# Masked attention, then an int8 linear layer: the last half in single steps, more row sums on the array, int8 loads in twos

## The chip, the cores and the metric

The kernel runs on one core of one Trainium2 chip. The time is the device time of one execution in microseconds (us); the median of three executions is compared. All stage times below are counted from the start of the span of one profiled execution. In the profile PE is the matrix engine (PEld its weight loads), DVE the vector engine, ACT the scalar engine, POOL the GpSimd engine and SP the queue from which this kernel issues nearly all of its transfers.

## The reference

`x` is (8, 512, 1024): 8 batches, 512 channels, 1024 positions. Cut to what matters, and with the int8 step written out:

```python
Q, K, V = (einsum('oc,bct->bto', W, x).reshape(B, T, 16, 32).transpose(0, 2, 1, 3) for W in (Wq, Wk, Wv))
att = einsum('bhqd,bhkd->bhqk', Q, K) / sqrt(32) + b[0]
att = softmax(att * m + (1 - m) * -1e30)          # m: 0/1 mask over the keys
y   = einsum('bhqk,bhkd->bhqd', att, V)           # back to (B, 512, 1024)
scale = max(abs(y).max(-1), 1e-7) / 127           # one scale for each row of 1024
q   = clip(round(y / scale), -128, 127)           # int8
out = x + (einsum('bsk,nk->bsn', q, weight) * scale * w_scale + bias).astype(float16)
```

So each of the 8 x 512 rows of the attention's result must be known over all its 1024 positions before it can be rounded, and only then can the linear layer (1024 in, 1024 out) of that row start.

## The kernel before

**Groups, halves, steps, pairs.** The work is cut into 32 groups (a batch and four of its 16 heads, that is 128 channels). A group has two halves of 512 queries, a half has 8 steps of 128 keys (kc 0 to 7), so there are 512 steps. The main loop (L783 to L844) runs over pairs of steps, 8 pairs p = 0 to 7 in a group i, with four pairs for each half. Nothing is reordered by a planner: the order in which the Python calls are made is the order on every engine's queue (`manual_schedule`), and the framework only adds the waits. Each queue is strictly in order, SP and POOL included.

**One step.** `scores(s)` (L407) makes 4 matmuls that spread the shift, which is the row maximum (L418), and 4 matmuls of keys by queries (L423) into two PSUM tiles from a pool `ps_s` of two buffers; ACT then takes the exponential of each of the two tiles (L432) into `e`, which has three buffers. `product(s)` (L450) multiplies the `e` of that step by the values into `av` (L457). The sum of the exponentials, the softmax denominator, is made by POOL: `add_up` (L437) adds one `e` after another into `sum` (7 adds in a half, L444), and matmuls with a matrix of ones add up its rows once a half (`half_denominators`, `add_rows`, L471 to L492). In the very last half the row sums are made on the array directly from each `e`, with no POOL add (`last_denominators`, L496).

**Pairs.** In a pair the order on PE is: scores of step s; then `product` of the two steps of the pair before; then scores of step s+1; then four units of `maxima` (L334), which find row maxima two halves ahead (PE makes 1024 scores for 128 queries, DVE takes their maximum, L375), with "pieces" of a job between them: projections of the groups ahead, or the linear layer of two groups back. Two of the four units use the buffers of `ps_s`, so they wait for ACT or DVE to free them. The maxima of a half are split into bf16 parts by POOL (`split_tops`, L389, five small instructions) and turned by a transposing DMA (`place_tops`, L398); the first shift matmul of that half needs this transfer.

**The int8 weights.** In groups 0 and 1 eight blocks of the weight matrix are loaded by SP (`load_ffn`, L151), one at the start of each of the pairs 0, 1, 4 and 5, and cast to bf16 by POOL two at a time at the start of the pairs 2 and 6 (`casts`, L157). On POOL the casts stand between adds of the sum; on SP the loads stand between the copies that build the operands of `maxima` (`stack_head`, L315) and the weight loads of the projections (`load_w`, L111). `load_w` of Wq is queued after pair 4's units and its first user is the first piece of pair 5.

**The end.** Group 31 is the last. Its maxima were all made by its pair 2. The linear layer of group 29 runs in its pairs 1 and 2, that of group 30 in its pairs 6 and 7. After the loop: row sums and products of the last two steps, division (four reciprocals on DVE, L510), the largest value, the scale, rounding of the two halves on ACT (two instructions each, L537 and L539), 8 transposes on PE (L578), clipping on DVE (L573), the linear layer of group 31 in two halves one after the other (L614), each followed by three DVE instructions (scale L626, bias L598, add `x` L599) and its store; both halves' `x` is loaded at the moment the half's first matmul is queued (L590).

Of the kernel before, what the change touches and what calls it, by code (L numbers as in the profile page):

```python
# [20 lines left out]
P = 128  # L21
# [11 lines left out]
def kernel(  # L33
# [49 lines left out]
    last = n_groups - 1  # L83
    SCALE = 1.0 / math.sqrt(DH)
# [352 lines left out]
    def add_up(s):  # L437
        X, kc = divmod(s, NT)
        if kc == 0 or X == n_halves - 1:
            return  # L440
        if kc == 1:
            sums[X] = work.tile([P, HG, HALF], F32, tag="sum", name=f"sum_{X}", bufs=2)
        other = exps[s - 1] if kc == 1 else sums[X]
        nc.gpsimd.tensor_tensor(sums[X], other, exps[s], ALU.add)  # L444
# [32 lines left out]
    def take_denominators(X, acc):  # L477
        dens[X] = work.tile([P, HALF], F32, tag="den", name=f"den_{X}")
        nc.vector.tensor_copy(dens[X], acc)

    def denominators(X):
        acc = bank(f"dps_{X}")
        add_rows(acc, sums.pop(X), True, True)
        take_denominators(X, acc)

# [8 lines left out]
    last_sum = []  # L494

    def last_denominators(s):  # L496

        kc = s % NT
        if kc == 0:
            last_sum.append(ps_m.tile([P, HALF], F32, tag="m", name="dps_last"))  # L500
        add_rows(last_sum[0], exps[s], kc == 0, kc == NT - 1)
        if kc == NT - 1:
            take_denominators(n_halves - 1, last_sum[0])
# [29 lines left out]
    def round_y(i, step, cols=slice(0, T)):  # L533
        inv, _, qt = quants[i]
        y = ys[i][:, cols]
        if step == 0:
            nc.scalar.activation(y, y, AF.Identity, bias=rounding[:, 0:1], scale=inv)  # L537
        else:
            nc.scalar.activation(qt[:, cols], y, AF.Identity, bias=rounding[:, 1:2])  # L539

    def quantise(i, step):
# [6 lines left out]
        if step == 1:  # L548
            nc.scalar.activation(y, y, AF.Identity, bias=rounding[:, 0:1], scale=inv)
            nc.scalar.activation(y, y, AF.Relu, bias=rounding[:, 2:3])  # L550
        else:
            nc.scalar.activation(y, y, AF.Relu, bias=rounding[:, 3:4], scale=-1.0)
# [12 lines left out]
    def last_turn(i):  # L565

        pieces = NH
        _, scale, qt = quants.pop(i)
        tr = bank(f"qtps_{i}", BF, (P, NT, P))
        qT = work.tile([P, NT, P], BF, tag="qT", name=f"qT_{i}")  # L570

        def rest(ks):
            nc.vector.tensor_scalar(qT[:, ks, :], tr[:, ks, :], -128.0, 127.0, ALU.max, ALU.min)  # L573

        for a in range(pieces):
            ks = slice(a * NT // pieces, (a + 1) * NT // pieces)
            for k in range(ks.start, ks.stop):
                nc.tensor.transpose(tr[:, k, :], qt[:, k * P : (k + 1) * P], ident)  # L578
            later.append(lambda ks=ks: rest(ks))
        outs[i] = qT, scale  # L580

    def linear(i, h, quarters=(0, 1), width=QUARTER):

        b, g = divmod(i, NG)
# [3 lines left out]
        def begin():  # L588
            xr = work.tile([P, HALF], F32, tag=f"xr{h}", name=f"xr_{i}_{h}")
            nc.sync.dma_start(xr, x[b, g * P : (g + 1) * P, half])  # L590
            o = work.tile([P, HALF], F32, tag=f"o{h}", name=f"o_{i}_{h}")
            o16 = work.tile([P, HALF], F16, tag=f"o16{h}", name=f"o16_{i}_{h}")
            residual[i, h] = xr, o, o16

        def finish():
            xr, o, o16 = residual.pop((i, h))
            engine = nc.vector if i == last else nc.gpsimd
            engine.tensor_tensor(o16, o, bias_sb[:, half], ALU.add)  # L598
            engine.tensor_tensor(o, o16, xr, ALU.add)  # L599
            store = lambda: nc.sync.dma_start(out[b, g * P : (g + 1) * P, half], o)  # L600
            if i == last:
                store()
            else:
                stores.append(store)

        def piece(a, r):
            if (i, h) not in residual:
                begin()
# [4 lines left out]
            for k in range(r * size, (r + 1) * size):  # L613
                nc.tensor.matmul(  # L614
# [16 lines left out]
            if a == HALF // width - 1:  # L631
                finishes.append(finish)

        return [lambda a=a, r=r: piece(a, r) for a in quarters for r in range(NT // size)]


# [30 lines left out]
    def job(i, p):  # L667


        if i == last:  # L670
            if p in (1, 2):
                return linear(i - 2, p - 1, (0,), HALF)
            if p in (6, 7):
                return linear(i - 1, p - 6, (0,), HALF)
            return []
# [27 lines left out]
    def after_units(i, p):  # L703

        flush(stores)
        if i == last:
            if p == 3:
                for step in range(HN):
                    normalise(2 * i - 1, step)
            if p == 4:  # L710
                normalise(2 * i - 1, 4)
                quantise(i - 1, 0)
                quantise(i - 1, 1)
            if p == 5:
                quantise(i - 1, 2)
# [61 lines left out]

    load_mask(0)
# [4 lines left out]
    for n in range(FIRST, n_pairs):  # L783
# [23 lines left out]
        if i in (0, 1) and p in (0, 1, 4, 5):  # L807
            load_ffn(i * HG + (0, 1, 4, 5).index(p))
# [3 lines left out]
        if n >= 1:  # L812
            for a in (s - 2, s - 1):
                if a >= n_steps - NT:
                    last_denominators(a)
                product(a)
# [5 lines left out]
        if p == 5 and i == last:  # L822
# [93 lines left out]
```

## Time and profile before

| | |
|---|---|
| Median of three executions | 2579.47 us (2577.87 to 2584.42) |
| Profiled execution: time | 2581.33 us |
| Profiled execution: span | 2579.5 us, granted PE clock 0.994 |
| PE busy | 2516.9 us, 98% |
| POOL busy | 2259.7 us, 88% |
| DVE busy | 1801.7 us, 70% |
| ACT busy | 1477.8 us, 57% |
| PE busy in the stretch 60 to 220 us | 145.45 of 160 us |
| PE busy in the stretch 500 to 2000 us | 1496.24 of 1500 us |
| PE busy in the stretch 2510 to 2556 us | 37.28 of 46 us, clock 0.89 |
| PE busy in the stretch 2556 to 2579.5 us | 6.78 of 23.5 us, clock 0.72 |

How to read it: PE is full in the middle of the run, from about 220 us to about 2510 us. It has gaps in groups 0 and 1 (60 to 220 us) and in the second half of group 31 with what follows (from 2510 us on). A line of the timeline has the start, the duration, the engine, the source line, the operation with its output and inputs, how many were merged, and in brackets how long the engine had been idle before it and what ended that wait.

### The profile page before, as it was taken

Reading aid. Unit: us, or ns where it says so; the run is one execution under the profiler, and the core shown is the slowest. Engines: PE = TensorE matmul, PEld = TensorE weight load, DVE = VectorE, ACT = ScalarE, POOL = GpSimd, SP = SyncE. Lnnn points to the kernel's source line nnn. Section 1 sums busy time; section 2 is a strip of 40 time slices with the busy share of each in tenths; the row PEclk is TensorE's granted clock in tenths of the full one; section 3 lists DMA queues with packets and bytes.
Section 4 is the critical chain, followed back from the end, with each engine's and each line's share of the span. In section 5 each row is a group of like instructions: output and inputs, shape, how many; then the busy total and the mean of one; then the engine's idle time right before and its main releaser. Section 6 shows DMA issues by size and latency. Waiting matters only on the chain. (4 is left out here: it accounts for less than half of the span.)

```text
span 2579.5 us, 50764 instructions
## 1 busy us (share of the span) xinstructions
PE 2516.9 (98%) x19390; PEld 1426.8 (55%) x19390; DVE 1801.7 (70%) x2886; ACT 1477.8 (57%) x1645; POOL 2259.7 (88%) x911
## 2 busy tenths in 40 slices
PE   8899999999999999999999999999999999999986
PEld 4455555555555555555555555555555555555531
DVE  4466777777777777777777777777777777777772
ACT  2445655565655656655656655656655566555553
POOL 1798899998999999899999999999899998999992
PEclk9999999999999999999999999999999999999998
DMA  4323433334333333334333343334333334233221
GB/s 130 104 54 81 113 84 90 78 84 121 78 83 97 88 100 91 76 91 116 80 80 94 83 115 88 77 79 104 104 86 86 76 88 125 75 87 85 73 54 43
DMA packets 225952, 228.08 MB, mean 88 GB/s; under 512 B 104368, under 2 KB 138160, under 8 KB 225712
## 3 DMA queue, kind: packets, MB, share of 16 engines
q1 hardware_dynamic: 225712, 224.85, 34.1%
q8 instruction: 155, 2.54, 0.4%
q14 instruction: 85, 0.70, 0.1%
HBM read 57.70 MB, written 16.78 MB: 29 GB/s over the span
## 5 line engine op out<-in xcount | busy, mean ns | idle before, releaser
L444 POOL TENSOR_TENSOR sum<-sum,e 128x2048 f32<-128x2048 f32 x378 | 1725.5, 4565 | 31.0 <-ACT e L432 11.8
L375 DVE CUSTOM_DVE_ANT_0 rest<-mps,row 128x1024 bf16<-128x1024 f32 x1024 | 1253.8, 1224 | 627.9 <-PE mps L344 390.6
L432 ACT ACTIVATE e<-sps,kbias 128x1024 f32<-128x1024 f32 x1024 | 1085.7, 1111 | 491.7 <-PE sps L423 468.2
L344 PE MATMUL mps<-ks,qs 128*128 128x512 f32 x2032 | 764.7, 457 | 9.1 <-ACT e L432 5.1
L423 PE MATMUL sps<-qf,kf 32*128 32x512 f32 x4096 | 552.3, 591 | 0.0
L457 PE MATMUL av<-e,v 128*32 128x512 f32 x4096 | 496.5, 602 | 0.0
L344 PEld LDWEIGHTS mps<-ks,qs 128*128 128x128 f32 x2032 | 332.7, 190 | 239.1 <-issue 96.7
L444 POOL TENSOR_TENSOR sum<-e,e 128x2048 f32<-128x2048 f32 x63 | 286.3, 4545 | 157.3 <-ACT e L432 147.0
L457 PEld LDWEIGHTS av<-e,v 128*32 128x32 f32 x4096 | 107.7, 109 | 350.0 <-issue 350.0
L293 PEld LDWEIGHTS job<-wv,x 128*128 128x128 f32 x1860 | 255.7, 191 | 27.5
L293 PE MATMUL job<-wv,x 128*128 128x128 f32 x1860 | 257.8, 274 | 0.0
L418 PE MATMUL sps<-shift,ones_b 32*128 32x512 bf16 x2048 | 233.8, 383 | 20.9 <-DMA shift<-part 11.1
L207 PE MATMUL job<-x,wq 128*128 128x256 f32 x900 | 245.0, 382 | 6.6 <-DMA wq<-in_wqT 6.2
L510 DVE RECIPROCAL den<-den 128x128 f32<-128x128 f32 x256 | 228.4, 925 | 0.0
L207 PE MATMUL job<-x,wk 128*128 128x256 f32 x854 | 223.8, 378 | 0.0
L423 PEld LDWEIGHTS sps<-qf,kf 32*128 32x128 f32 x4096 | 207.8, 184 | 4.4
L207 PEld LDWEIGHTS job<-x,wq 128*128 128x128 f32 x900 | 169.6, 190 | 45.1 <-DMA wq<-in_wqT 12.4
L301 ACT COPY v<-job 128x256 f32<-128x256 f32 (+1 forms) x93 | 41.3, 444 | 251.0 <-PE job L293 251.0
L418 PEld LDWEIGHTS <-ones_b 32*128 32x128 bf16 x2048 | 69.8, 91 | 204.2 <-issue 176.7
L207 PEld LDWEIGHTS job<-x,wk 128*128 128x128 f32 x854 | 161.2, 189 | 30.8
L236 ACT ACTIVATE qh<-job,top 128x256 fp32r<-128x256 f32 (+1 forms) x84 | 47.9, 570 | 170.5 <-PE job L207 169.3
L614 PE MATMUL job<-w_sb,qT 128*128 128x256 bf16 (+1 forms) x960 | 133.0, 278 | 0.0
(97 smaller groups left out, 1429.8 us busy)
## 6 DMA issues: line engine op xcount, KB each, us to landing
ks<-kh SPq DMA_DIRECT2D x512, 64.0 KB, 2.0
ks<-kl SPq DMA_DIRECT2D x512, 64.0 KB, 2.0
qs<-qh SPq DMA_DIRECT2D x508, 64.0 KB, 2.0
qs<-ql SPq DMA_DIRECT2D x508, 64.0 KB, 2.0
x<-in_x SPq DMA_DIRECT2D x32, 512.0 KB, 4.7
xr<-in_x SPq DMA_DIRECT2D x64, 256.0 KB, 3.4
out<-o SPq DMA_DIRECT2D x64, 256.0 KB, 3.4
wk<-in_wkT SPq DMA_DIRECT2D x32, 256.0 KB, 3.7
```

Of the source, the lines that this page charges most:

```text
L207: matmul(acc[:, place], w[:, c, :], x_sb[b, c][:, h * HALF : (h + 1) * HALF][:, cols], start=(c == 0), stop=(c == NG - 1),)
L236: nc.scalar.activation(dst, acc, AF.Copy, scale=top)
L293: matmul(acc[:, place : place + P], x_sb[b, c][:, k * P : (k + 1) * P], wv_sb[:, c, g * P : (g + 1) * P], start=(c == 0), stop=(c == NG - 1),)
L344: nc.tensor.matmul(acc[:, a, :], q[:, n0 * P : (n0 + 1) * P], kk[:, a * HALF : (a + 1) * HALF], start=True, stop=True,)
L375: nc.vector.tensor_tensor_reduce(out=rest, in0=acc.rearrange("p h t -> p (h t)"), in1=row, scale=-1.0, scalar=HIGH, op0=ALU.add, op1=ALU.m ...
L418: nc.tensor.matmul(accs[j // 2][:, j % 2, :], ones_b[r, :], shift[r, :], start=True, stop=False)
L423: nc.tensor.matmul(accs[j // 2][:, j % 2, :], k[r, k0 * P : (k0 + 1) * P], q[r, :], start=False, stop=True,)
L432: nc.scalar.activation(e[:, 2 * a : 2 * a + 2, :], acc, AF.Exp, bias=kbias[:, kc : kc + 1], scale=SCALE)
L444: nc.gpsimd.tensor_tensor(sums[X], other, exps[s], ALU.add)
L457: nc.tensor.matmul(accs_av[X][r, :], v_sb[i][:, kc, r], exps[s][:, j, :], start=(kc == 0), stop=(kc == NT - 1),)
L510: nc.vector.reciprocal(piece, piece)
L614: nc.tensor.matmul(acc, qT[:, k, :], w8_sb[:, k, half][:, cols], start=(k == 0), stop=(k == NT - 1),)
```

## The change

1. **Int8 loads in twos.** The blocks are loaded two at a time, at the start of the pairs 0 and 4 of groups 0 and 1, instead of one each at 0, 1, 4 and 5. The casts stay where they were.
2. **Row sums on the array from 12 steps before the end** (`ON_ARRAY`). Steps kc 4 to 7 of the last but one half no longer go through POOL's adds: four adds of POOL go, and four more `add_rows` (4 matmuls each) come. The partial sum of kc 0 to 3 is put on the array first and these are added to it.
3. **Single steps at the end.** From pair 3 of the last group on, the row sums and products of a step follow the scores of the next step (`sum_up`), instead of two steps at once in the next pair.
4. **Last group's other work.** The linear layer of group 29 moves from pairs 1 and 2 to pairs 0 and 1. The last half of group 30 is normalised, and the rounding of that group started, one pair earlier, in four single ACT steps spread over pairs 4 and 5. The linear layer of group 30 stays in pairs 6 and 7, its matmuls cut into four with 32 output rows each (`columns`, 64 instead of 16), between the steps: the first output half entire after pair 6, the second in two parts in pair 7.
5. **The very end over two engines.** One half is rounded on ACT and the other on DVE; transposes start with DVE's half; each half has its own PSUM tile; both output halves of the linear layer are accumulated side by side, in the order of the transposed chunks; `x` is loaded ahead for both; bias and `x` of the first output half are added by POOL, of the second by DVE; the two stores are issued after that.
6. **Pieces after the second unit.** In a pair with four or fewer pieces the first unit of `maxima` is no longer followed by a piece: the second unit comes directly after the first, then two pieces. This concerns the pairs 1, 2, 5 and 6 of groups 0 and 1, pair 5 of groups 2, 6, 10 and so on to 30, and pairs 0 and 1 of the last group.

```diff
+    ON_ARRAY = n_steps - NT - HN
 ...
     def add_up(s):
         X, kc = divmod(s, NT)
-        if kc == 0 or X == n_halves - 1:
+        if kc == 0 or s >= ON_ARRAY:
             return
 ...
     def last_denominators(s):
+        X, kc = divmod(s, NT)
+        if s < ON_ARRAY:
+            return
+        whole = X == n_halves - 1
+        if X not in last_sums:
+            if whole:
+                last_sums[X] = ps_m.tile([P, HALF], F32, tag="m", name=f"dps_{X}")
+            else:
+                last_sums[X] = bank(f"dps_{X}")
+                add_rows(last_sums[X], sums[X], True, False)
+        acc = last_sums[X]
+        add_rows(acc, exps[s], whole and kc == 0, kc == NT - 1)
 ...
+    def round_half(i, h):
+        inv, _, qt = quants[i]
+        cols = slice(h * HALF, (h + 1) * HALF)
+        y = ys[i][:, cols]
+        if h == 0:
+            nc.scalar.activation(y, y, AF.Identity, bias=rounding[:, 0:1], scale=inv)
+            nc.scalar.activation(qt[:, cols], y, AF.Identity, bias=rounding[:, 1:2])
+        else:
+            nc.vector.tensor_scalar(y, y, inv, ROUND, ALU.mult, ALU.add)
+            nc.vector.tensor_scalar(qt[:, cols], y, -ROUND, None, ALU.add)
 ...
+    def last_linear(i):
+        _, scale, qt = quants.pop(i)
+        qT = work.tile([P, NT, P], BF, tag="qT", name=f"qT_{i}")
+        chunks = [range(NT // 2, NT), range(NT // 2)]
+        for ks in chunks:
+            tr = ps_s.tile([P, NT // 2, P], BF, tag="s", name=f"qtps_{i}_{ks.start}")
+            for k in ks:
+                nc.tensor.transpose(tr[:, k - ks.start, :], qt[:, k * P : (k + 1) * P], ident)
+            nc.vector.tensor_scalar(
+                qT[:, ks.start : ks.stop, :], tr, -128.0, 127.0, ALU.max, ALU.min
+            )
+        accs = [bank(f"job_{i}"), ps_m.tile([P, HALF], F32, tag="m", name=f"job_{i}_1")]
+        for ks in chunks:
+            for h in range(NH):
+                for k in ks:
+                    nc.tensor.matmul(
+                        accs[h],
+                        qT[:, k, :],
+                        w8_sb[:, k, h * HALF : (h + 1) * HALF],
+                        start=(k == chunks[0].start),
+                        stop=(k == chunks[1].stop - 1),
+                    )
+        for h in range(NH):
+            half = slice(h * HALF, (h + 1) * HALF)
+            nc.vector.scalar_tensor_tensor(
+                residual[i, h][1], accs[h], scale, ws_sb[:, half], ALU.mult, ALU.mult
+            )
+        for h, engine in ((0, nc.gpsimd), (1, nc.vector)):
+            add_residual(i, h, engine)
+        flush(stores)
 ...
     def job(i, p):
         if i == last:
-            if p in (1, 2):
-                return linear(i - 2, p - 1, (0,), HALF)
-            if p in (6, 7):
-                return linear(i - 1, p - 6, (0,), HALF)
-            return []
+            return linear(i - 2, p, (0,), HALF) if p < 2 else []
 ...
+    def sum_up(end):
+        for a in range(summed[0], max(summed[0], end)):
+            last_denominators(a)
+            product(a)
+            summed[0] = a + 1
+
+    def open_linear(i, h):
+        jobs["bank"] = bank(f"job_{i}_{h}")
+        jobs["linear"] = linear(i, h, (0,), HALF)
+
+    def run_linear(number):
+        for _ in range(number):
+            jobs["linear"].pop(0)(columns)
 ...
-        if i in (0, 1) and p in (0, 1, 4, 5):
-            load_ffn(i * HG + (0, 1, 4, 5).index(p))
+        if i in (0, 1) and p in (0, 4):
+            for a in range(2):
+                load_ffn(i * HG + p // 2 + a)
         if n >= 0:
             scores(s)
             add_up(s)
-        if n >= 1:
-            for a in (s - 2, s - 1):
-                if a >= n_steps - NT:
-                    last_denominators(a)
-                product(a)
+            if i == last and p in (4, 5):
+                quantise(i - 1, 2 * p - 7)
+        sum_up(s)
 ...
+        if n == n_pairs - 1:
+            open_linear(last - 1, 1)
+            run_linear(2)
 ...
+            if i == last and p in (4, 5):
+                quantise(i - 1, 2 * p - 6)
+            if i == last and p >= HN - 1:
+                sum_up(s + 1)
+            if n == n_pairs - 2:
+                open_linear(last - 1, 0)
+                run_linear(4)
+            if n == n_pairs - 1:
+                run_linear(2)
 ...
-            for _ in range(-(-len(pieces) // (HN - a))):
-                pieces.pop(0)()
+            if a > 0 or len(pieces) > NG:
+                for _ in range(-(-len(pieces) // (HN - a))):
+                    pieces.pop(0)()
 ...
     for h in range(NH):
-        for step in range(2):
-            round_y(last, step, slice(h * HALF, (h + 1) * HALF))
-    last_turn(last)
-    flush(later)
-    for h in range(NH):
-        jobs["bank"] = bank(f"job_last_{h}")
-        for piece in linear(last, h, (0,), HALF):
-            piece()
-        flush(later)
-        flush(finishes)
+        round_half(last, h)
+    last_linear(last)
```

## The prediction, made before the changed kernel ran

> **What bounds the kernel now.** I read the busy shares first: PE 98%, POOL 88%. The answer by stages then shows PE full from 220 to 2510 us, so time can be won only where it has gaps: in groups 0 and 1, in the last half, and behind it. A gap closed in front of a full engine stays won. First, POOL's timeline of group 0:
>
> ```profile
> 79.84 1.04 POOL L157 CAST w_sb<-w8raw 128x1024 bf16<-128x1024 int8 x1
> 87.16 1.04 POOL L157 CAST w_sb<-w8raw 128x1024 bf16<-128x1024 int8 x1 [6.28 <-DMA w8raw<-in_w8T]
> 88.16 9.18 POOL L444 TENSOR_TENSOR sum<-sum,e 128x2048 f32<-128x2048 f32 x2
> 97.28 0.27 POOL L394 CAST part<-tops 128x16 bf16<-128x16 f32 x1
> ...
> 129.71 1.04 POOL L157 CAST w_sb<-w8raw 128x1024 bf16<-128x1024 int8 x1 [3.20 <-DMA w8raw<-in_w8T]
> ```
>
> The second cast waits 6.28 us for a load that SP issued late (84.76, behind a row of copies); the adds and the split of the maxima (97.28) stand behind it. PE's timeline of groups 0 and 1 shows who pays:
>
> ```profile
> 93.91 0.73 PE L344 MATMUL mps<-ks,qs 128*128 128x512 f32 x2 [1.61 <-ACT e L432]
> ...
> 101.34 0.40 PE L418 MATMUL sps<-shift,ones_b 32*128 32x512 bf16 x4 [3.54 <-DMA shift<-part]
> 101.56 1.41 PE L423 MATMUL sps<-qf,kf 32*128 32x512 f32 x8
> 102.91 3.18 PE L457 MATMUL av<-e,v 128*32 128x512 f32 x16
> ...
> 144.75 0.39 PE L418 MATMUL sps<-shift,ones_b 32*128 32x512 bf16 x4 [2.59 <-DMA shift<-part]
> ...
> 201.80 1.22 PE L207 MATMUL job<-x,wq 128*128 128x256 f32 x2 [3.25 <-DMA wq<-in_wqT]
> ```
>
> At 93.91 it waits for ACT, which waits 3.36 for a free `e` that POOL holds; at 101.34 and 144.75 for the shift; and after 101.34 the array is slow: two products take 3.18, elsewhere 1.92. The timeline of the end:
>
> ```profile
> 2503.17 9.17 POOL L444 TENSOR_TENSOR sum<-sum,e 128x2048 f32<-128x2048 f32 x2
> ...
> 2512.27 0.27 POOL L394 CAST part<-tops 128x16 bf16<-128x16 f32 x1
> ...
> 2516.59 0.61 PE L418 MATMUL sps<-shift,ones_b 32*128 32x512 bf16 x4 [4.95 <-DMA shift<-part]
> ...
> 2518.84 3.53 PE L457 MATMUL av<-e,v 128*32 128x512 f32 x16
> ...
> 2575.71 0.69 DVE L599 TENSOR_TENSOR o<-o,xr 128x512 f32<-128x512 f16 x1 [1.21 <-DMA xr<-in_x]
> ```
>
> The maxima were ready at 2508.3 (last one 2507.07 + 1.23), but POOL added until 2512.3; PE stood 4.95 and went slow. The chain of waits ends with the second load of `x`, 2.73 us.
>
> **The change part by part.** All durations are of the profiled execution: 2581.33 us, a span of 2579.5; it lies 1.9 above the median shown.
>
> *A. Loads in twos.* Each second load now follows the first, a pair before its cast, so the three cast waits (6.28, 3.20, 5.87) go. First: PE's 1.61 + 3.54 go, and the slow stretch (101.34 to 105.92 is 4.58; the same work from 144.75 took 2.92), 1.66: -6.8. PE would reach this shift at 96.2; the shift, 6.28 earlier, lands at 95.1, covered by 1.1. Second: the 2.59 goes, as POOL would split at 130.6 (ACT's `e`, two casts and two adds summed) and the shift land at 135.5, with PE there at 136.0. This cover is 0.5; without it PE waits for what is missing. Third: no PE wait hung on it, 0.
>
> Against it: in pair 4 the second load stands on SP in front of Wq, 0.68 us (115.31 to 115.99). In group 0 Wq would be issued at 110.4 and land, 3.04 later, at 113.4; PE has its second unit done at 112.5 and waits 0.9. Before, Wq began at 119.03 without that unit (0.57): the gain is 6.2, so 0.6 of the 6.8 is given back. In group 1 Wq lands 0.68 later with 0.57 done before: +0.1. There slow matmuls followed the 3.25: 6.21 from 201.80 to 208.01, where the next pair needs 3.71, so 2.5. The new wait is 2.8; one of 2.59 was not followed by slow matmuls, one of 3.25 was; between them I take half, -1.2 (ends 0, -2.5). At pair 0 SP's copies move back by 0.6, for operands used a pair later: 0. Sum of A: -6.2 - 2.6 + 0.1 - 1.2 = -9.9, ends -4 and -12.
>
> The Trainium skill (TensorE: Matmul & The Clock Gate, "What's actually happening") has the array's clock halved after an idle window of about 3.4 us. The row with 3.25 went slow below that. By the rule alone the wait of 2.8 would stay fast and A would be -11.1.
>
> *B. Last half.* Four adds of 4.57 leave POOL. In its new order it is free by 2505, so the split starts when DVE is done, at 2508.4, and the shift lands at 2512.7. PE in pair 3: scores of kc 6 end at 2508.3; five blocks (row sums of kc 0 to 3; row sums and product of kc 4 and of kc 5) at 0.93 each (two products take 1.86, 2508.16 to 2510.02) end at 2513.0; with kc 7's scores and kc 6's two blocks the key matmuls of the last half start at 2516.75, before at 2516.99. So the new row sums are paid by the stall, and what is won comes after: no slow array, and single steps. A step costs PE 1.17 (key matmuls to next block, 2506.99 to 2508.16) + 1.86 + 0.38 (shift) = 3.41, and the loop through ACT 1.24 + 2.12 + 0.05 = 3.41. Group 30's rounding (1.15 to 1.24 a step) fits into the 1.3 in which ACT waits for key matmuls, but for the first, which shares it with a copy of 0.59: +0.6. Before, a pair took 8.2 to 9.9 (shift matmuls at 2531.44, 2541.30, 2549.51). kc 5 then starts at 2534.4. Group 30's linear layer: 8 matmuls took 1.83 (2542.48 to 2544.31); quartered, the nearest row is a projection cut the same way, 0.55 against 0.38 whole, so 1.83 to 2.65; I take 2.0 twice, as those four ran beside each other. Last row sum at 2549.2 against 2555.3: -6.1. With 0.5 more in each step -1; with nothing lost -7.5.
>
> Group 29's linear layer moves to pair 0, which DVE holds (PE waits 0.99 for it at 2488.06): 0.2, contained above. Its operand, issued at 2478.18 with 3.1 to landing, is there by 2485.
>
> *C. The end.* From the row sum to the first rounding (T) the chain stays, 6.7 us on DVE. Rounding on DVE has no row; 0.42 (clipping, 512 columns) to 0.69 (copy, 512), I take 0.55, twice 1.1, beside ACT's 0.81 + 0.72. Two groups of transposes, 0.61 each, with clipping under the second: the linear layer starts at T + 2.5, before at T + 4.55. It needs 3.5 slow and 1.9 fast, without the gap of 0.9: T + 7.9. The scale takes 0.75 each, T + 8.6. POOL adds the first half from T + 7.7 (1.29 + 1.49), DVE the second beside it; DVE's product of two SBUF operands (L513) takes 0.80 in the median and 1.54 at most, the latter beside such POOL adds. So DVE ends between T + 10.0 and T + 11.7, I take 11.2; then store 0.33 and 2.7 to the span's end: T + 14.2, before T + 17.4. Gain 3.2, ends 2 and 4.5. `x` comes early, and the store of group 30 in front of it on SP is out by then.
>
> The Trainium skill (GPSIMD Engine Reference, "Specifications") says that POOL and DVE contend for SBUF when DVE has two SBUF inputs, which speaks against two engines at the very end; L513's 1.54 agrees. By the rule alone both adds are slow, T + 11.7, and C is -2.7.
>
> *D. Pieces after the second unit.* 18 pairs. The second unit waits for ACT (0.16 to 0.61) with or without a piece before it; the piece moves behind, and DVE's four maxima (1.38 apart) set the pair's end. 0.1 each, +1.5; at most a whole piece (0.43) each, +7.7; a gain only at Wq, counted in A.
>
> Sum: -9.9 - 6.1 - 3.2 + 1.5 = -17.7: 2563.6 for the profiled execution, 2561.8 against the median.
>
> **Rivals.**
>
> *1. Wq takes the place of the cast waits.* Behind two loads, it becomes PE's wait in both groups, with a slow array each time. For it: the 3.25; SP issues without a pause from the shift to Wq (98.83 to 115.99). Against: most of that lateness came from POOL. A falls to -2: 2569.7.
>
> *2. The quartered linear layer runs in series.* 64 matmuls at 0.23 are 14.6 instead of 4.0: 2572.4. Against: the quartered projection at 0.55.
>
> *3. Slower: the array stays slow in the last half.* For it: 3.53 for two products at 2518.84, and a clock of 0.89 from 2510 to 2556. A step then takes 2.25 + 3.5 = 5.7, 2.3 more; from eight slow steps on it eats the 17.7, and twelve give +27.6: 2589. Against: in the new order PE idles hardly 0.3 us a step.
>
> *4. The change does only half of A and B,* through covers that fail by little: 2570.
>
> **How the numbers follow.** Likeliest case 0.66, own range 2555 to 2568; a gain beyond it 0.03; rivals 1 to 4: 0.10, 0.05, 0.05, 0.11. About 0.3% (7.7 us, 2571.7) is what can be told from no change. Faster: likeliest, beyond, rival 1 and half of 4: 0.84. Same: rival 2 and half of 4: 0.11. Slower: rival 3, 0.05. The range 2551 to 2573 reaches from the good ends of A, B and C to rival 2.
>
> **What would show it.** Right: casts of the int8 blocks without a wait; no PE wait at the first two shifts; the last half's split right behind DVE's last maximum; steps of 3.4 to 3.5; first rounding 14.2 before the span's end. Wrong: waits for Wq above 3 us, products of a step above 1.2, steps of 4 and more, or DVE's last adds above 1.5 each.

## The result and the profile after

| | before | changed |
|---|---|---|
| Median, measured together | 2581.85 us (2577.87 to 2584.42, 4 executions) | 2563.93 us (2561.76 to 2566.11, 4) |
| Ratio | | 0.9932, 95% interval 0.9913 to 0.9951 |
| Profiled execution: time, span | 2581.33, 2579.5 us | 2566.11, 2564.3 us |
| PE busy, 60 to 220 us | 145.45 of 160 us | 149.69 of 160 us |

The changed kernel is 0.68% faster; forecast were 17.7 of 2579.5 us, 0.69%. The profiled execution is the slowest of its four, which matters below.

To place the gain I use one landmark that both kernels have 64 times: ACT's copy of `av` into `y` at the end of each half. How much earlier it stands than in the profiled execution of before is called the lead here. It is 6.6 us after half 0, 7.9 after half 3 (the end of group 1), 3.3 after half 61 (the end of group 30), 11.5 after half 63, and 15.2 at the end of the span. So groups 0 and 1 gave 7.9, the long middle took 4.6 away, the last two halves gave 8.2 and the end 3.7.

POOL's timeline of groups 0 and 1 in the changed kernel:

```profile
79.48 2.03 POOL L158 CAST w_sb<-w8raw 128x1024 bf16<-128x1024 int8 x2
...
90.58 0.26 POOL L395 CAST part<-tops 128x16 bf16<-128x16 f32 x1
...
118.74 2.02 POOL L158 CAST w_sb<-w8raw 128x1024 bf16<-128x1024 int8 x2
```

The casts come two in a row and wait for nothing; the split of the maxima stands at 90.58 instead of 97.28. PE's timeline of the same groups, and of group 5 (the bracket is how long PE stood idle before, and for what):

```profile
96.25 0.40 PE L419 MATMUL sps<-shift,ones_b 32*128 32x512 bf16 x4 [0.69 <-DMA shift<-part]
...
114.69 1.99 PE L208 MATMUL job<-x,wq 128*128 128x256 f32 x4 [1.93 <-DMA wq<-in_wqT]
116.12 1.42 PE L345 MATMUL mps<-ks,qs 128*128 128x512 f32 x2
...
195.68 1.13 PE L208 MATMUL job<-x,wq 128*128 128x256 f32 x4 [2.12 <-DMA wq<-in_wqT]
...
510.51 1.86 PE L208 MATMUL job<-x,wq 128*128 128x256 f32 x4 [2.09 <-DMA wq<-in_wqT]
```

Of the 3.54 for the first shift 0.69 is left, of the 2.59 for the second nothing. In their place stand waits for Wq of about 2 us, and behind each the array is slow for a while (two matmuls of `maxima`, elsewhere 0.73 together, take 1.42). At the one at 510.51 most of the lead lost in the middle goes: 3.7 of the 4.6 us, within one half. POOL's timeline in front of the last half:

```profile
2505.48 0.25 POOL L395 CAST part<-tops 128x16 bf16<-128x16 f32 x1 [3.61 <-DVE tops L376]
```

PE's timeline of the last half: the row sums and the product of one step, and the first half of the linear layer of group 30:

```profile
2514.41 1.07 PE L474 MATMUL dps<-e,ones_f 128*32 128x512 f32 x8
2515.29 1.04 PE L458 MATMUL av<-e,v 128*32 128x512 f32 x8
...
2533.24 1.91 PE L197 MATMUL job<-w_sb,qT 128*32 128x512 bf16 x32
```

POOL now waits for DVE's last maximum and splits 0.07 behind its end (2505.41); PE has no wait for the shift there. The key matmuls of kc 0 to 5 follow one another by 3.35 to 3.62 us. Half of the quartered linear layer (32 matmuls with 32 output rows each) takes 1.9 us. DVE's timeline of the end:

```profile
2550.59 0.49 DVE L543 TENSOR_SCALAR y<-y,inv 128x512 f32<-128x512 f32 x1
2551.11 0.43 DVE L544 TENSOR_SCALAR qt<-y 128x512 bf16<-128x512 f32 x1
...
2556.86 1.61 DVE L598 SCALAR_TENSOR_TENSOR o<-job,scale,ws_sb 128x512 f32<-128x512 f32 x2 [3.57 <-PE job L589]
2558.51 0.99 DVE L618 TENSOR_TENSOR o<-o,bias_sb 128x512 f16<-128x512 f32 x1
2559.53 1.53 DVE L619 TENSOR_TENSOR o<-o,xr 128x512 f32<-128x512 f16 x1
```

The first rounding (T) is at 2550.59, and the span ends 13.7 behind it, before it was 17.4.

### The profile page after: what moved, and what is told of

It reads as the page before. It is cut to its first block, busy times and chain, and to the rows that moved or that the text cites. A ratio compares the mean times of both kernels' runs of the same rounds, so it can differ in the third digit from the quotient of the medians.

```text
span 2564.3 us, 50906 instructions
## 1 busy us (share of the span) xinstructions
PE 2511.0 (98%) x19467; PEld 1428.2 (56%) x19470; DVE 1803.3 (70%) x2886; ACT 1476.1 (58%) x1643; POOL 2243.1 (87%) x909
## 4 chain that ended last, share of the span: by engine, by line
PE 70%; POOL 17%; SPq 3%; issue 3%; DMA 2%; ACT 2%; DVE 1%; POOLq 0%; DVEq 0%; ACTq 0%
PE mps L345 15%; POOL sum L445 15%; PE av L458 13%; PE sps L424 13%; PE job L208 11%; PE job L294 6%; PE sps L419 5%; SPq L322 3%; PE job L635 3%; PE dps L474 2%; PE job L197 2%; ACT e L433 1%; DMA wq<-in_wqT 1%; POOL o L619 1%; POOL o L618 1%
## 5 line engine op out<-in xcount | busy, mean ns | idle before, releaser
L445 POOL TENSOR_TENSOR sum<-sum,e 128x2048 f32<-128x2048 f32 x374 | 1706.7, 4563 | 37.4 <-ACT e L433 18.4
L345 PE MATMUL mps<-ks,qs 128*128 128x512 f32 x2032 | 765.5, 458 | 15.4 <-ACT e L433 12.1
L294 PEld LDWEIGHTS job<-wv,x 128*128 128x128 f32 x1860 | 255.1, 191 | 27.2
L208 PEld LDWEIGHTS job<-x,wq 128*128 128x128 f32 x900 | 170.6, 191 | 45.5 <-DMA wq<-in_wqT 12.3
L635 PE MATMUL job<-w_sb,qT 128*128 128x256 bf16 (+1 forms) x942 | 127.0, 276 | 0.1
```

The source lines that it names most:

```text
L208: matmul(acc[:, place], w[:, c, :], x_sb[b, c][:, h * HALF : (h + 1) * HALF][:, cols], start=(c == 0), stop=(c == NG - 1),)
L294: matmul(acc[:, place : place + P], x_sb[b, c][:, k * P : (k + 1) * P], wv_sb[:, c, g * P : (g + 1) * P], start=(c == 0), stop=(c == NG - 1),)
L345: nc.tensor.matmul(acc[:, a, :], q[:, n0 * P : (n0 + 1) * P], kk[:, a * HALF : (a + 1) * HALF], start=True, stop=True,)
L635: matmul(acc, qT[:, k, :], w8_sb[:, k, half][:, cols], start=(k == 0), stop=(k == NT - 1),)
```

## The experiments

My theory was the prediction's: the four parts are worth what they were put at, and each gain stays. Against it stood that the waits for Wq eat part A (rival 1), that the last half gains by something else than single steps, and, once the middle had lost 4.6 us, that the order of the pieces (D) costs more than thought. The leads of all executions, in us, each against the same profiled execution of before:

| kernel | half 0 | end of group 1 | end of group 30 | half 63 | end of span |
|---|---|---|---|---|---|
| changed | 6.6 | 7.9 | 3.3 | 11.5 | 15.2 |
| changed, once more (e12_same) | 5.9 | 9.2 | 10.6 | 18.8 | 22.0 |
| e1_loads_apart | 0.4 | 1.8 | 2.9 | 11.1 | 14.7 |
| e2_loads_only | 6.3 | 6.8 | 6.8 | 7.3 | 7.7 |
| e3_pieces_old | 5.3 | 6.8 | 7.2 | 15.4 | 19.4 |
| e4_wq_first | 6.5 | 14.1 | 13.7 | 21.8 | 25.9 |
| e5_pairs | 5.5 | 6.8 | 7.8 | 9.9 | 12.3 |
| e6_two_back | 3.7 | 7.6 | 6.4 | 12.3 | 16.2 |
| e8_adds_on_dve | 4.7 | 11.3 | 12.8 | 21.0 | 24.1 |
| e9_wq_early | 5.7 | 14.6 | 18.7 | 26.8 | 30.9 |
| e11_both | 5.2 | 14.0 | 18.2 | 26.4 | 31.5 |
| e10_both_old_pieces | 6.0 | 14.8 | 18.9 | 27.2 | 32.3 |

### The changed kernel with the old loads

```diff
-        if i in (0, 1) and p in (0, 4):
-            for a in range(2):
-                load_ffn(i * HG + p // 2 + a)
+        if i in (0, 1) and p in (0, 1, 4, 5):
+            load_ffn(i * HG + (0, 1, 4, 5).index(p))
```

> The changed kernel with the int8 loads as before (pairs 0, 1, 4, 5), everything else new. My theory: the cast waits return (6.3, 3.2 and about 6 us on POOL), the first shift waits about 3.5 us again, and of the lead of 7.9 us over the kernel before at the end of group 1 nothing is left but the effect of the piece order on Wq, 0 to 1 us. Total 7 to 8 us above the changed kernel, about 2571. Rival (the lead comes from the order of pieces, which gives Wq more time): the lead at the end of group 1 stays above 4 us and the total rises by less than 4.

2569.02 us (2566.65 to 2571.48), beside 2578.92 for before: ratio 0.9962 (0.9948 to 0.9977). The waits of before are back (1.43 for ACT, 3.51 and 3.08 for the shifts), and the lead at the end of group 1 is 1.8 instead of 7.9. So the loads are worth 6.1 by these two traces (one each; identical code is seen further down to differ between 6.8 and 11.3 there). The 1.8 is put down to the pieces, the only other change in groups 0 and 1, which let PE reach Wq with more work done: there is no wait for Wq in group 0 (0.86 in the kernel before), and the one in group 1 is 1.43 instead of 3.25, with a slow array behind it all the same. PE's timeline of that kernel:

```profile
144.21 0.39 PE L419 MATMUL sps<-shift,ones_b 32*128 32x512 bf16 x4 [3.08 <-DMA shift<-part]
...
145.39 1.93 PE L458 MATMUL av<-e,v 128*32 128x512 f32 x16
...
200.73 2.05 PE L208 MATMUL job<-x,wq 128*128 128x256 f32 x4 [1.43 <-DMA wq<-in_wqT]
202.22 1.42 PE L345 MATMUL mps<-ks,qs 128*128 128x512 f32 x2
```

A wait of 3.08 leaves the array fast (two products in 1.93), one of 1.43 makes it slow. Length alone cannot decide it; this led to the measurement of the gaps below.

### The kernel before with the loads in twos

```diff
-        if i in (0, 1) and p in (0, 1, 4, 5):
-            load_ffn(i * HG + (0, 1, 4, 5).index(p))
+        if i in (0, 1) and p in (0, 4):
+            for a in range(2):
+                load_ffn(i * HG + p // 2 + a)
```

> The kernel before with only the loads in twos. My theory: no cast waits, no wait of PE for the first two shifts, a lead of 6.5 to 7.5 us over the kernel before at the end of group 1, total about 2574. Wq is waited for longer than in the changed kernel (2.5 to 3.5 us in both groups), since the first piece stands before the second unit. Rival (Wq takes the place of the cast waits): lead below 3 us.

2575.15 us (2569.65 to 2576.93), ratio 0.998 (0.9971 to 0.9989). The casts wait no longer, the lead after half 0 is 6.3, as in the changed kernel. But the waits for Wq become 3.18 and 3.47, both with a slow array, so that only 6.8 is there at the end of group 1 and 7.7 at the end of the span.

### The changed kernel with the old order of pieces

```diff
-            if a > 0 or len(pieces) > NG:
-                for _ in range(-(-len(pieces) // (HN - a))):
-                    pieces.pop(0)()
+            for _ in range(-(-len(pieces) // (HN - a))):
+                pieces.pop(0)()
```

> The changed kernel with a piece after the first unit again. My forecast had the new order costing 0.1 us in each of 18 pairs, 1.5 in all, and helping only at Wq in groups 0 and 1 (0.57 each). Then this run is 0.5 us faster to 1 us slower than the changed kernel, which its time cannot tell; in the traces the lead at the end of group 1 is 0.5 to 1.5 us smaller and the stretch from group 2 to group 30 is 0.5 to 1.5 us shorter. Rival (the order of pieces is what lost 4.6 us between groups 2 and 30 in the profiled execution): that stretch is 4 us or more shorter, and no loss of 3.7 us stands at half 11. If that loss is a late landing of one Wq load by chance, it stands elsewhere or nowhere here.

2562.54 us (2561.91 to 2567.61), ratio 0.9937 (0.992 to 0.9955): not to be told from the changed kernel. Its waits for Wq are 3.72 and 3.04, against 1.93 and 2.12. In group 0, 1.1 of the difference is a later landing (5.12 after the issue, 4.01 in the changed kernel), so the new order shortens the two waits by 0.7 and 0.9; the prediction had 0.57 in part A. Between the ends of group 1 and 30 it wins 0.5, where the changed kernel lost 4.6; whether the order or chance did that, this run alone could not tell.

### Wq in front of the int8 loads

```diff
-        if i in (0, 1) and p in (0, 4):
+        if i in (0, 1) and p == 0:
             for a in range(2):
-                load_ffn(i * HG + p // 2 + a)
+                load_ffn(i * HG + a)
...
                 load_w(i + 2, 0)
+            if i in (0, 1):
+                for a in range(2):
+                    load_ffn(i * HG + 2 + a)
```

> The changed kernel with the two int8 loads of pair 4 issued right behind the load of Wq instead of in front of it. My theory: the two loads in front of Wq cost PE 1.9 and 2.1 us of waiting and the slow matmuls behind that. Wq is issued 1.2 us earlier and lands alone, in 3.0 instead of 4.0 us in group 0; the waits fall below 0.5 us, no slow matmuls follow, and the lead at the end of group 1 grows from 7.9 to 11 to 13 us; total 3 to 5 us below the changed kernel, about 2560. Rival (PE waits for Wq because SP reaches it late whatever stands in front): the waits stay above 1.2 us and the lead grows by less than 2.

2557.46 us (2554.26 to 2560.72), ratio 0.9913 (0.9895 to 0.9932). Wq is issued at 109.56 instead of 110.64, PE has no wait above 0.5 for it in group 0 and 1.18 in group 1, and no part of groups 0 and 1 is at a lower clock. The lead at the end of group 1 is 14.1: 6.2 us more than in the changed kernel, and 5.5 more than the mean of the five executions of its code further down, from about 1 us of queue. The wait left in group 1, at 1.18, is longer than the 0.5 that was expected.

### Pairs instead of single steps

```diff
-            if i == last and p >= HN - 1:
-                sum_up(s + 1)
```

> Changed kernel, but in the last half the row sums and products again run in pairs (two scores, then two steps' sums and products). Theory (single steps carry most of the gain in the last half): the second scores of a pair are followed at once by the next pair's, which wait for ACT; PE idles about 2.2 us at four boundaries (kc 7 to 0, 1 to 2, 3 to 4, 5 to 6), of which the quartered linear layer fills some 3: the last half takes about 4.5 us longer (3.5 to 8, more if a window of the array clock goes slow), 2568 against 2564. Rival (the gain came from the array sums in front of the half and the single steps only reorder): under 1 us longer.

2569.02 us (2566.37 to 2571.71), beside 2578.86 for before: ratio 0.9961 (0.9948 to 0.9974). From the end of half 61 to the end of half 63 it gains 2.0 us on before, the changed kernel 8.2. So the single steps are worth 6.2, within the 3.5 to 8 of the theory. PE's timeline of that kernel shows where:

```profile
2507.66 0.39 PE L419 MATMUL sps<-shift,ones_b 32*128 32x512 bf16 x2 [1.27 <-ACT e L433]
2508.67 0.39 PE L419 MATMUL sps<-shift,ones_b 32*128 32x512 bf16 x2 [0.61 <-ACT e L433]
...
2515.95 0.39 PE L419 MATMUL sps<-shift,ones_b 32*128 32x512 bf16 x2 [1.27 <-ACT e L433]
2516.95 0.39 PE L419 MATMUL sps<-shift,ones_b 32*128 32x512 bf16 x2 [0.61 <-ACT e L433]
```

At each of three boundaries between pairs PE waits 1.21 to 1.27 and then 0.61 for ACT to empty the score tiles; a pair takes 8.28 (2505.37 to 2513.65 between key matmuls), where two single steps take 6.8. The third boundary leaves its window of the array clock 1.82 idle, and the next one, from 2525.38, is at half clock, which by an estimate (half of 3.41) costs 1.7 of the 6.2. The fourth boundary goes to the linear layer, which fills it.

### Two of the four adds back on POOL

```diff
-    ON_ARRAY = n_steps - NT - HN
+    ON_ARRAY = n_steps - NT - 2
```

> Changed kernel, but kc 4 and kc 5 of the last half but one are summed by POOL again; kc 6 and 7 stay on the array. Theory (these adds held the split of the maxima): POOL finishes the two adds about 4.1 us after DVE's last maximum, the split moves from 0.15 to about 4 us behind it, the shift lands about 4 later; PE has 1.9 us of row sums less and waits about 2.7 us for it; the last half begins 0.9 later, or up to 2.6 later when a window of the array clock goes slow. Rival (the adds were harmless, the row sums are only cost): no wait for the shift, 1.9 us faster.

2564.52 us (2562.53 to 2565.74), ratio 0.9943 (0.9926 to 0.996). POOL's timeline of that kernel:

```profile
2498.72 9.16 POOL L445 TENSOR_TENSOR sum<-sum,e 128x2048 f32<-128x2048 f32 x2
2507.81 0.73 POOL L395 CAST part<-tops 128x16 bf16<-128x16 f32 x1
```

PE's timeline of the same kernel:

```profile
2507.93 1.07 PE L474 MATMUL dps<-sum,ones_f 128*32 128x512 f32 x8 [2.30 <-POOL sum L445]
...
2512.28 0.40 PE L419 MATMUL sps<-shift,ones_b 32*128 32x512 bf16 x4 [1.56 <-DMA shift<-part]
```

The split follows the adds, as the theory says, and PE waits 1.56 for the shift, after 2.30 for POOL's sum, a wait that I had not listed. The last two halves gain 6.0 instead of 8.2: the two adds cost 2.2, the upper part of the expected 0.9 to 2.6. No part of the half is at a lower clock. The rival (1.9 faster) falls.

### Both last additions on DVE

```diff
-        for h, engine in ((0, nc.gpsimd), (1, nc.vector)):
+        for h, engine in ((0, nc.vector), (1, nc.vector)):
```

> Changed kernel, but at the very end DVE makes the bias and residual additions of both halves (POOL none). Theory (POOL beside DVE slows DVE's 0.69 to 0.99 and 1.53, and the split in two is worth about nothing): four adds of about 0.7 behind the two scales, so DVE ends 0.3 us later than now, 2564 within 0.5 in the trace. Rival (two engines are worth the forecast share): over 1 us later.

2560.91 us (2557.22 to 2562.4), ratio 0.9929 (0.9914 to 0.9943). Its end, on DVE:

```profile
2548.05 1.61 DVE L598 SCALAR_TENSOR_TENSOR o<-job,scale,ws_sb 128x512 f32<-128x512 f32 x2 [4.26 <-PE job L589]
2549.58 0.68 DVE L618 TENSOR_TENSOR o<-o,bias_sb 128x512 f16<-128x512 f32 x1
...
2551.63 0.69 DVE L619 TENSOR_TENSOR o<-o,xr 128x512 f32<-128x512 f16 x1
```

From the first scale to DVE's last addition it is 4.27 us, in the changed kernel 4.20 (2556.86 to 2561.06): four additions of 0.69 on one engine cost the same as 0.99 + 1.53 on DVE beside POOL's 1.26 + 1.49. The split over two engines is worth 0.07. (Up to there this kernel is the changed one; its longer lead comes from groups 0 and 1, 3.4 us, and from the middle, 6.1.)

### The array clock by itself

All of the kernel is replaced by stretches of products with a gap after each:

```diff
+            for _ in range(54 + (r * 5 + a * 3) % 16):
+                nc.tensor.matmul(acc, w, mov[:, :HALF], start=True, stop=True)
+            nc.scalar.copy(mov[:, :c], src[:, :c])
```

> A measurement of the array clock alone: nothing of the reference is computed; dense stretches of 54 to 69 bf16 products of 128x512 on the array, and between them 70 gaps of ten lengths (about 0.8 to 3 us) in which PE waits for a copy by ACT; the output is a copy of part of x. Theory (the clock is set anew in fixed windows of 3.413 us, and a window that is idle for more than about 1.9 us makes the next one slow): every slow stretch lasts a multiple of 3.41 us, all of them begin on one grid, gaps under 1.8 never lead to one, gaps from 2.0 to 3.4 do in some positions and not in others, and the idle part of the window before tells which. Rival (the length of a gap decides): one threshold of length separates all gaps, and the slow stretches begin at any time.

The granted clock, read in slices of 0.25 us, falls to half 18 times in 1100 us, each time for 3.41 us or, twice, for 6.83, and all 18 beginnings lie on one grid of 3.413 us to within 0.01 us. The windows of one such case, with PE's busy time (second number) and the granted clock (the last number but two):

```profile
118.49:121.90 3.41, 1.16 (x7) 0.40 (x6) 0.00 (x0) 2.11 (x1) 0.00 (x0) 1.00 0.00 0
121.90:125.31 3.41, 3.41 (x10) 1.21 (x9) 0.00 (x0) 0.00 (x0) 0.00 (x0) 0.50 0.00 0
125.31:128.73 3.42, 3.42 (x17) 1.56 (x16) 0.00 (x0) 0.00 (x0) 0.00 (x0) 1.00 0.00 0
```

A window with 2.25 idle is followed by one in which 10 products are done instead of 17. With the grid laid over the 69 gaps, every window at full clock that was idle for 2.01 us or more is followed by a slow one, none with 1.99 or less is. Which gaps are concerned depends on where they lie:

| gap | its parts in one window and the next | the window behind the larger part |
|---|---|---|
| 2.04 (737.30 to 739.34) | 2.04 and 0 | slow |
| 2.05 (264.22 to 266.27) | 1.04 and 1.01 | full |
| 2.58 (135.82 to 138.40) | 2.58 and 0 | slow |
| 2.58 (936.98 to 939.56) | 0.71 and 1.87 | full |
| 3.24 (487.47 to 490.71) | 3.07 and 0.17 | slow |
| 3.26 (809.86 to 813.12) | 1.53 and 1.73 | full |

The rival with one length falls. The same grid fits the kernels: in the execution of before, the slow stretches begin at 102.08 and 201.07, 29.0 windows apart, in the changed one at 114.81 and 196.73, 24.0 apart. In e1_loads_apart the 3.08 at 144.21 is cut into 1.65 and 1.44; the 1.43 before 200.73 shares its window with an earlier 0.56 and ends it, 1.99 idle. In groups 0 and 1 of all these kernels, windows with up to 1.83 idle stay without consequence and those from 1.89 on do not; in the last half 1.82 was enough three times (before, e2_loads_only, e5_pairs), and behind it, in e8_adds_on_dve, 1.84 was not enough twice. So in the kernels the limit lies near 1.8 to 1.9; either the idle share alone does not settle every window there, or the ends of the matmuls, which the profile models, blur it by that much.

### The changed kernel once more, and Wq early

The first is without an edit:

> The changed kernel as it is, once more beside the next three, to see how far its executions differ in groups 0 and 1. Theory (the waits for Wq are there each time, but whether one makes a window of the array clock slow depends on where the free windows lie): lead over before at the end of group 1 between 6 and 11.5 us, slow windows behind zero, one or two of the waits for Wq, time 2561 to 2566. Rival (one execution stands for all): lead 7.9 within 0.3, slow windows behind both waits.

2560.1 us (2559.32 to 2569.17, 6 executions), beside 2579.8 for before: ratio 0.993 (0.9917 to 0.9944); the time is 0.9 under the expected 2561 to 2566. Waits for Wq of 1.94 and 1.75; only the first is followed by a slow window (2.43 idle in the window before it; 1.74 at the second). The lead is 9.2 at the end of group 1, and nothing is lost in the middle. Five executions of kernels whose code is the same up to the last group (changed, e12_same, e5_pairs, e6_two_back, e8_adds_on_dve) have 7.9, 9.2, 6.8, 7.6 and 11.3 at the end of group 1, with two, one, two, one and no slow window in groups 0 and 1.

For the second, the copies of the fourth head's rows go behind the load of Wq in every group:

```diff
-        if p in (7, 0, 3) and group(ahead) and ahead > 0:
+        if p in (7, 0) + ((3,) if i < 0 else ()) and group(ahead) and ahead > 0:
...
                 load_w(i + 2, 0)
+            if i >= 0:
+                for which, h in ((1, 0), (0, 0), (1, 1)):
+                    stack_head(i + 1, 3, which, h)
```

> Changed kernel, but in every group the 12 copies of the fourth head's key and query rows go behind the load of Wq on SP's queue and not ahead of it; the int8 loads stay in twos in front of it. Theory (SP reaches Wq too late, with a cover of about nothing in all groups): Wq is issued about 3 us earlier, just behind the last use of the old Wq, and lands before PE wants it; no wait for Wq above 0.5 in groups 0 and 1, no slow window there, lead at the end of group 1 about 13 to 14 us instead of 6 to 11.5, no loss of 1 us or more at a group's Wq later on; time 2556 to 2559. Rival (the copies that now come later are the next wait): PE waits for the fourth head's rows in pair 6, the lead is no more than 10.

2551.43 us (2550.38 to 2552.6), ratio 0.9887 (0.9875 to 0.99), which is 4.6 under the expected 2556 to 2559. SP's timeline in group 0, of the changed kernel:

```profile
110.64 0.38 SPq L116 DMA_DIRECT2D wq<-in_wqT  x1
```

and of this one:

```profile
107.02 0.38 SPq L116 DMA_DIRECT2D wq<-in_wqT  x1
```

PE's timeline there:

```profile
112.92 0.74 PE L345 MATMUL mps<-ks,qs 128*128 128x512 f32 x2 [0.56 <-ACT e L433]
113.49 0.81 PE L208 MATMUL job<-x,wq 128*128 128x256 f32 x3
```

Wq is issued 3.6 earlier, and no wait for Wq is left in the whole trace; the execution of before has 7 (6.21 us in sum), that of the changed kernel 8 (8.31). No window from 60 us to the last products is slow, the lead at the end of group 1 is 14.6, and it grows by another 4.1 in the middle, which had not been expected. Of these 4.1 before spends 2.1 on waits for Wq; where the other 2 come from is open. The rival (the late copies) falls: in groups 0 and 1 PE waits for no copy of these rows that the edit moves.

### Products that nobody reads, and the pieces once more

```diff
+    busy = ps_s.tile([P, HALF], F32, tag="s", name="busy")
+    for _ in range(28):
+        nc.tensor.matmul(busy, ident, w8_sb[:, 0, :HALF], start=True, stop=True)
     for step in range(5):
         normalise(2 * last + 1, step)
```

> The last kernel with 28 products on the array whose result nobody reads, between the last product of the attention and the transposes, where PE otherwise idles 6.9 us. Theory (those idle windows make the clock slow for transposes and linear layer): no slow window after them; the first scale starts 1.6 us earlier against the row sum, the stretch from the last copy by ACT to the end of the span is 17.5 to 18.2 us instead of 19.2 to 20.2; time 1.6 under the last kernel's. Rival (the end is bound by DVE and the store): 0.3 or less.

2549.6 us (2548.74 to 2549.85), ratio 0.9879 (0.9867 to 0.9892), 1.8 under e9_wq_early. PE's timeline of the end, in e9_wq_early:

```profile
2537.38 4.50 PE L589 MATMUL job<-w_sb,qT 128*128 128x512 bf16 x16
```

and in this kernel:

```profile
2529.73 6.22 PE L901 MATMUL busy<-w_sb,ident 128*128 128x512 bf16 x28
2536.72 0.40 PE L581 MATMUL qtps<-ident,qt 128*128 128x128 bf16 x4 [0.78 <-DVE qt L544]
...
2537.64 3.63 PE L589 MATMUL job<-w_sb,qT 128*128 128x512 bf16 x16
```

DVE's timeline there:

```profile
2540.50 1.61 DVE L598 SCALAR_TENSOR_TENSOR o<-job,scale,ws_sb 128x512 f32<-128x512 f32 x2 [2.30 <-PE job L589]
```

The 16 matmuls take 3.63, against 4.50 in e9_wq_early and 5.41 in e12_same, and the stretch from ACT's last copy to the end of the span is 18.1 us (19.2 and 20.1). From the first of the 28 products to the last of the 16 matmuls no window is slow. The gain in the trace is 1.1, not the expected 1.6, since in e9_wq_early the linear layer took 4.50 and not the 4.89 (2552.73 to 2557.62) from which the expectation was worked out.

With the old order of the pieces on top (the edit of e3_pieces_old):

> The kernel before this one, with the order of pieces and units as in the kernel before (a piece also in front of the first unit of a pair), in all groups. Theory (once no wait for Wq is there, the place of the pieces costs or wins about nothing, since DVE's maxima set the pair): within 1 us of the kernel with the new order. The prediction's own term says 1.5 us faster with the old order; a rival says slower, by 1 or more, because PE then reaches the second unit later.

2549.35 us (2548.97 to 2549.86), ratio 0.9879 (0.9866 to 0.9892). From the end of group 1 to the end of group 30 it gains 4.07, with the new order 4.11; from the end of half 0 to the end of group 1 both gain 8.89, and in the half with the first pairs of the last group 1.57 and 1.56. The order of the pieces costs nothing.

## Why the prediction was right, and where it was not

**The total** is right to within 2.1 us, and the steps of B, C and most of A are seen as they were told. That it comes so close is in part luck. By the traces, A gave about 1.3 less than forecast (in the mean of five), B 2.1 more, C up to 0.9 more, and D cost nothing instead of 1.5; against this stand losses in the middle that no term had, 4.6 in the profiled execution. The same code measured again (e12_same) is 19.7 us under the kernel before, and not 17.9.

**A, loads in twos: forecast -9.9, measured -6.8 to -11.3, in the mean of five executions -8.6** (of which, by e1_loads_apart, up to 1.8 is the pieces' share, which the forecast counted here too). The casts without a wait and the two shifts are as forecast; the cover of the first shift was 0.7 short instead of 1.1 long. The step that failed is the new wait for Wq in group 0: "lands, 3.04 later", a wait of 0.9 with a fast array. It took 4.05 from its issue to the matmul that waits for it (4.07, 3.89 and 3.79 in e12_same, e5_pairs and e6_two_back), the waits of these four executions were 1.68 to 1.94, that is the 0.9 and about 1 of later landing, and each filled its window enough to make the next one slow, 1.7 us of work. What made it land later is open: in the fifth, e8_adds_on_dve, it landed in 2.84 and PE did not wait, and in group 1 it landed in 3.0 to 3.3, behind the same two int8 loads each time. In group 1 the waits were 1.57 to 2.25 (e8_adds_on_dve: 1.96), below the forecast 2.8. Rival 1 thus came half true, and e4_wq_first and e9_wq_early show its price: about 6 us of a possible 14.

**The slow stretch** was put at one half, by the lengths of the waits (2.59 fast, 3.25 slow). That is the wrong rule. Laid on the grid, the 2.59 of before had 1.71 in one window and the 3.25 had 2.53 in its. The page that I cited (the Trainium skill, TensorE: Matmul & The Clock Gate, "What's actually happening") also says that the window is 3413 ns and free-running, and the trace agrees (3.413 us, 18 beginnings on one grid). I used only its "idle window" (and A without the slow stretch is -11.2 by the prediction's own terms, not -11.1). An entirely idle window is not needed: 2.01 of 3.41 us was enough.

**B, last half: forecast -6.1, measured -8.2,** the same in all nine executions that have it whole. The steps are 3.35 to 3.62 for 3.41, and the key matmuls of the half begin 0.25 earlier than forecast (2513.24 and the lead of 3.26, for 2516.75). The term that was mis-sized is the quartered linear layer, twice 2.0 us: it takes 1.9 and twice 0.97, but lengthens its steps only by 1.57, 0.49 and 0.97, because a part runs in PE's wait for ACT. That is 1.0 of the 2.1; another 0.4 is the copy that shares ACT with the first rounding, put at 0.6 and seen as 0.2 (a step of 3.62 for 3.41). With the 0.25 of the start this makes 1.7; the rest is spread over steps of 3.35 and the end of the chain. By the two experiments, single steps are worth 6.2 (with the slow window that pairs bring) and two of the four adds 2.2. Rivals 2 (in series) and 3 (slow array) fell: 32 quartered matmuls took 1.91, and the row sums and the product of a step no more than 1.07 each.

**C, the end: forecast -3.2, measured -3.2 to -4.1** in the executions that share the last step and this end, by how much of the linear layer falls into a slow window (the 16 matmuls take 4.5 to 5.4). The first rounding stands 13.7 before the span's end, forecast 14.2. The mechanism of the two engines was priced rightly as contention (DVE 0.99 and 1.53 beside POOL), but it brings nothing: 0.07 us. (The 1.53 passes the 1.5 that was named as a sign of being wrong; the sum had allowed for up to 1.54.) By the timelines C gains by the rounding on two engines, by transposes and clipping in two tiles and by the early load of `x`; these were not tried one by one.

**D, pieces: forecast +1.5, measured 0.0** (4.07 against 4.11 over the middle). "0.1 each" was a price without a row. The place of the pieces changes how long PE is seen waiting for ACT, in the middle 6.1 us with the new order (e11_both) and 1.7 with the old, at the same total. That DVE's maxima set these pairs' ends in both orders is what I take from this; no run tries it alone.

**The 4.6 lost in the middle of the profiled execution** are in no step of the forecast. 3.7 of them are a wait for Wq in group 5, in a window with 2.09 idle, followed by a slow one; of the four other executions of the same code three gain 1.0 to 1.5 in the middle, and one loses 1.3 (2.47 for Wq in group 5). In these two Wq landed 4.67 and 4.93 after its issue there, in the other three 2.7 to 3.6; why is open. The cover for Wq is about zero in every group, so that a late landing is paid in full; the prediction looked at it in groups 0 and 1 alone.

## What to carry to other kernels

When a stall is closed, the next transfer on the same in-order queue comes due earlier by as much; look up its cover in every stage before counting the gain, and put the transfer with no cover in front of the ones that have some (here 12 copies behind one load: 8.7 us, 2560.1 against 2551.43). Price a PE idle stretch by the share of its clock window that it fills, not by its length; two short waits in one window can cost more than a long one over two. And take more than one execution where covers are near zero: the same code differed by 9.5 us at the end of group 30 between two traces.

## What the runs showed that I had not expected

- The array clock is set in free windows of 3.413 us; 2.0 us of idleness in one (in e7_gaps; 1.8 to 1.9 in the kernels) halves the clock in the next, wherever the gap begins. A window that is already slow stayed slow with only 1.10 us of idleness (647.55 to 654.38 us in e7_gaps) and with 0.73 (201.07 to 207.89 us in before), while one with 0.89 did not (2558.63 in e2_loads_only); what decides there is open.
- The version that beats both kernels is the changed one with Wq ahead of the fourth head's copies and 28 unread products at the end: 2549.6 us, ratio 0.9879 to before, where the change itself has 0.993.
